# A two-layer graph attention kernel: the unmasked attention by running sums over sources sorted by f2, through DRAM by indirect DMA, in place of the 1024x1024 product

## The chip, the cores and the metric

The kernel runs on one core of one Trainium2 chip. The metric is device time in microseconds (us) of one execution. The kernel before takes 3468.1 us (median of three runs, 3465.04 to 3478.11).

## The reference, cut to what matters

There are 16 batches of 1024 nodes with 256 features, all in f32, and one adjacency matrix `adj` (1024x1024) for all. A batch passes three attentions: one unmasked inside the first layer, 512 features wide, and two masked ones, 256 wide. The unmasked one is the place of the change.

```python
def _gat(inp, adj_mask, W, a):                       # ALPHA = 0.2
    h = jnp.matmul(inp, W)
    f1 = jnp.matmul(h, a[:F_, 0])
    f2 = jnp.matmul(h, a[F_:, 0])
    e = jax.nn.leaky_relu(f1[:, :, None] + f2[:, None, :], ALPHA)
    if adj_mask is not None:
        e = jnp.where(adj_mask[None, :, :] > 0, e, NEG_INF)
    att = jax.nn.softmax(e, axis=2)
    h_prime = jnp.einsum('bij,bjf->bif', att, h)
    return jax.nn.elu(h_prime)
# layer 0, on h = relu(layernorm(x))
out = relu(h @ mlp1_w + mlp1_b)
residual = out
out = _gat(relu(out), None, W_fc, a_fc)              # unmasked, 512 wide
out = elu(out) + residual
out = relu(out @ mlp2_w + mlp2_b)
residual = out
out = _gat(relu(out), adj, W_hand, a_hand)           # masked, 256 wide
x = x + relu(elu(out) + residual)
# layer 1: x = x + relu(masked attention of relu(layernorm(x)), slope 0.01)
```

Target node i weighs source j by exp(leaky_relu(f1[i] + f2[j])). This is exp(f1+f2) where the sum is positive and exp(0.2(f1+f2)) where it isn't; each of the two is a product of a factor of i and a factor of j.

## The kernel before

A batch is held whole on the core: 1024 nodes are 8 tiles of 128 partitions (NT = 8), or 2 halves of 512 columns (NH = 2). The loop over the batches is unrolled, and the order in which an engine takes its instructions is made by the framework's scheduler from the order in which the source names them and from what is ready; it is fixed in the program. In the order of the source, batch b does this:

- `dense_attention` (L191) is the unmasked attention. It spreads f2 over all partitions by eight transposes on TensorE (`r2d`, L185), forms the row factors (`rows`) and, for each half of the targets, eight 128x512 weight tiles: ScalarE scales a row (`wd`, L222), VectorE takes the larger of the two products (`attd`, L224), and adds the tiles up for the softmax's denominator (`part`, L229). TensorE multiplies them with h (`acc`, L238): 4 chunks of 128 features by 8 sources by 2 halves. The result comes out with features on partitions, so the ELU chain (L257 to L263) adds straight into `resT`, which has that layout.
- `mlp2` (L356), `project` (`hm`, L272) and the transposes back to nodes on partitions (`on`, L368).
- `norm_transpose` and `mlp1` of batch b+1 (`nt`, L177; `m`, L329).
- `masked_attention` "a" (factors L281 to L305, weight tiles `att_a` L310, products `o_a` L318) with `finish_gnn0`, in which VectorE, ScalarE and GpSimd (`pos` L384, `e` L385) take part.
- `project_fc` of batch b+1 in two halves (`h`, L345), and between them `norm_transpose` and `project` of the second layer.
- `masked_attention` "b" (`att_b`, `o_b`) with `finish_gnn1`, whose adds are on GpSimd (L395), and the stores of the result from SyncE.

A call of an f32 matmul leaves two MATMUL records in the trace, a transpose one. DMAs are few: x in, the result out, both on SyncE's queue. GpSimd issues none.

## Time and profile before

| | |
|---|---|
| median of three runs | 3468.1 us |
| the profiled execution, its own time | 3473.71 us |
| its span (first to last instruction) | 3471.8 us |
| granted TensorE clock, mean | 0.970 |
| busy: TensorE | 3226.7 us (93%) |
| busy: VectorE, ScalarE, GpSimd | 1471.1 us (42%), 1218.5 us (35%), 375.6 us (11%) |
| moved by DMA | 43.56 MB, mean 13 GB/s |
| one batch in the steady state (two starts of `mlp2`, 1003.26 and 1216.72 us) | 213.46 us |

The busy shares are of the span. The execution's own time is 1.9 us over its span, the work around the first and the last instruction. The trace also gives the busy time in any stretch, the instructions of an engine in order of time with the idle time ahead of each in brackets, and the chain of work that ended last. Matmul ends are modelled, so matmul times here are taken from the distance of starts.

### The profile page before, as it was taken

Reading aid. Unit: us, or ns where it says so; the run is one execution under the profiler, and the core shown is the slowest. Engines: PE = TensorE matmul, PEld = TensorE weight load, DVE = VectorE, ACT = ScalarE, POOL = GpSimd, SP = SyncE. Lnnn points to the kernel's source line nnn. Section 1 sums busy time; section 2 is a strip of 40 time slices with the busy share of each in tenths; the row PEclk is TensorE's granted clock in tenths of the full one; section 3 lists DMA queues with packets and bytes.
Section 4 is the critical chain, followed back from the end, with each engine's and each line's share of the span. In section 5 each row is a group of like instructions: output and inputs, shape, how many; then the busy total and the mean of one; then the engine's idle time right before and its main releaser. Section 6 shows DMA issues by size and latency. Waiting matters only on the chain.

```text
span 3471.8 us, 32194 instructions
## 1 busy us (share of the span) xinstructions
PE 3226.7 (93%) x12161; PEld 2181.4 (63%) x12161; DVE 1471.1 (42%) x3425; ACT 1218.5 (35%) x2417; POOL 375.6 (11%) x486
## 2 busy tenths in 40 slices
PE   8899999999999999999999999999999999999997
PEld 5476574756747567475665847658476574756756
DVE  4635334353334534345343353533535334353343
ACT  3233333333333333333333334333333333333332
POOL 0010010111101111020100201101011010111102
PEclk9899999999999999999999999999999999999998
DMA  2100000000000000000000000000000000000000
GB/s 67 49 1 25 1 25 0 1 25 0 25 0 1 25 1 25 0 1 25 1 25 0 7 19 1 25 1 7 18 1 25 0 25 0 1 25 1 13 0 14
DMA packets 39635, 43.56 MB, mean 13 GB/s; under 512 B 1968, under 2 KB 36784, under 8 KB 39472
## 3 DMA queue, kind: packets, MB, share of 16 engines
q1 hardware_dynamic: 39472, 41.43, 3.6%
q8 instruction: 98, 1.61, 0.2%
q14 instruction: 65, 0.53, 0.1%
HBM read 24.64 MB, written 16.78 MB: 12 GB/s over the span
## 4 chain that ended last, share of the span: by engine, by line
PE 77%; DVE 10%; ACT 8%; POOL 2%; issue 2%; DMA 0%; ACTq 0%; POOLq 0%; DVEq 0%
PE acc L238 25%; PE o_b L318 13%; PE h L345 11%; PE m L329 6%; PE hm L272 6%; PE m L356 6%; PE o_a L318 4%; POOL e L385 2%; PE nt L177 2%; DVE att_a L310 2%; ACT pos L381 2%; PE rows L185 2%; DVE e L379 1%; ACT e L383 1%; DVE stats L163 1%
## 5 line engine op out<-in xcount | busy, mean ns | idle before, releaser
L238 PE MATMUL acc<-attd,hnat 128*128 128x512 f32 x2048 | 912.1, 602 | 0.2
L238 PEld LDWEIGHTS acc<-attd,hnat 128*128 128x128 f32 x2048 | 389.5, 194 | 464.2 <-issue 416.4
L318 PE MATMUL o_a<-hm,att_a 128*128 128x257 f32 x2048 | 478.6, 398 | 35.1 <-DVE att_a L310 35.1
L318 PEld LDWEIGHTS o_a<-hm,att_a 128*128 128x128 f32 x2048 | 408.4, 200 | 103.0 <-DVE att_a L310 39.2
L345 PE MATMUL h<-wfc_sb,resT 128*128 128x257 f32 x2048 | 453.0, 380 | 12.5 <-ACT pos L381 12.5
L318 PE MATMUL o_b<-hm,att_b 128*128 128x257 f32 x2048 | 452.9, 383 | 2.1 <-DVE att_b L310 2.1
L345 PEld LDWEIGHTS h<-wfc_sb,resT 128*128 128x128 f32 x2048 | 385.3, 189 | 75.6 <-ACT pos L381 18.6
L318 PEld LDWEIGHTS o_b<-hm,att_b 128*128 128x128 f32 x2048 | 386.6, 191 | 64.4 <-issue 4.5
L384 POOL TENSOR_TENSOR pos<-pos,onat 128x256 f32<-128x256 f32 x128 | 100.9, 789 | 1652.8 <-ACT pos L381 1505.4
L260 ACT ACTIVATE e<-e 128x512 f32<-128x512 f32 x128 | 80.7, 631 | 436.3 <-DVE e L259 436.3
L329 PE MATMUL m<-hT,w_sb 128*128 128x512 f32 x512 | 233.3, 604 | 0.0
L356 PE MATMUL m<-resT,w_sb 128*128 128x512 f32 x512 | 222.8, 592 | 0.0
L224 DVE SCALAR_TENSOR_TENSOR attd<-rowsd,bd,wd 128x512 f32<-128x512 f32 x256 | 185.7, 746 | 67.6 <-ACT wd L222 67.6
L310 DVE SCALAR_TENSOR_TENSOR att_a<-rows_a,qwd_a,edge 128x512 f32<-128x512 f32 x256 | 198.4, 831 | 31.2 <-ACT rows_a L303 31.2
L222 ACT ACTIVATE wd<-rowsd,bd 128x512 f32<-128x512 f32 x256 | 179.4, 720 | 71.2 <-DVE attd L224 70.7
L395 POOL TENSOR_TENSOR x<-x,r 128x256 f32<-128x256 f32 x128 | 109.3, 854 | 851.5 <-ACT r L394 851.5
L310 DVE SCALAR_TENSOR_TENSOR att_b<-rows_b,qwd_b,edge 128x512 f32<-128x512 f32 x256 | 188.3, 802 | 29.8 <-ACT rows_b L303 29.8
L381 ACT ACTIVATE pos<-o_a,rec 128x256 f32<-128x256 f32 x128 | 60.6, 473 | 394.2 <-DVE e L379 353.6
L394 ACT ACTIVATE r<-o_b,rec 128x256 f32<-128x256 f32 x128 | 60.6, 473 | 382.4 <-DVE rec L392 382.4
L347 ACT COPY hnat<-h 128x257 f32<-128x257 f32 x256 | 92.2, 373 | 273.1 <-PE h L345 273.1
L174 DVE TENSOR_SCALAR hn<-x,mv,rstd 128x256 f32<-128x256 f32 x256 | 95.8, 410 | 208.0 <-PE nt L177 152.7
L356 PEld LDWEIGHTS m<-resT,w_sb 128*128 128x128 f32 x512 | 97.1, 190 | 121.5 <-issue 121.5
(130 smaller groups left out, 2963.1 us busy)
## 6 DMA issues: line engine op xcount, KB each, us to landing
x<-in_x_dram SPq DMA_DIRECT2D x16, 1024.0 KB, 5.2
out_dram<-x SPq DMA_DIRECT2D x32, 512.0 KB, 2.9
adj_t<-in_adj_dram SPq DMA_DIRECT2D x16, 256.0 KB, 2.7
w_sb<-in_L_gnn_mlp_w_dram SPq DMA_DIRECT2D x2, 512.0 KB, 6.8
wfc_sb<-in_L_gnn_W_fc_dram SPq DMA_DIRECT2D x2, 512.0 KB, 6.8
wfc_sb_a<-in_L_gnn_a_fc_dram SPq DMA_DIRECT2D x1, 512.0 KB, 7.4
wh_sb<-in_L_gnn_W_hand_dram SPq DMA_DIRECT2D x1, 256.0 KB, 7.0
wl_sb<-in_L_gnn_W_dram SPq DMA_DIRECT2D x1, 256.0 KB, 7.2
```

What stands on the lines that cost most here:

```text
L222: nc.scalar.activation(w, rows[:, 1, :], AF.Copy, scale=bd[:, 1, j:j + 1])
L224: nc.vector.scalar_tensor_tensor(a_t, rows[:, 0, :], bd[:, 0, j:j + 1], w, op0=OP.mult, op1=OP.max)
L238: nc.tensor.matmul(accs[c], lhsT=h_nat[:, j, c // 2, lo:lo + P], rhs=att[j], start=(j == 0), stop=(j == NT - 1))
L272: nc.tensor.matmul(ps[:, :2 + F], lhsT=hT[:, c, t * P:(t + 1) * P], rhs=w_sb[:, c, 0, :], start=(c == 0), stop=(c == kc - 1))
L310: nc.vector.scalar_tensor_tensor(a_t, rows[:, h * HALF:(h + 1) * HALF], qwd[:, 1, j:j + 1], edge[:, j, h * HALF:(h + 1) * HALF], op0=OP.ma ...
L318: nc.tensor.matmul(ps[:, :F + 1], lhsT=att[j][:, u * P:(u + 1) * P], rhs=hm[:, j, 2:], start=(j == 0), stop=(j == NT - 1))
L329: nc.tensor.matmul(ps, lhsT=w1_sb[:, kc, c * P:(c + 1) * P], rhs=hT[:, kc, h * HALF:(h + 1) * HALF], start=(kc == 0), stop=(kc == FC - 1))
L345: nc.tensor.matmul(ps[:, :F + 1], lhsT=resT[:, kc, t * P:(t + 1) * P], rhs=wfc_sb[:, kc, g, :], start=(kc == 0), stop=(kc == HC - 1))
L356: nc.tensor.matmul(ps, lhsT=w2_sb[:, kc, c * P:(c + 1) * P], rhs=resT[:, kc, h * HALF:(h + 1) * HALF], start=(kc == 0), stop=(kc == HC - 1))
L381: nc.scalar.activation(pos, ps[:, :F], AF.Relu, scale=rec)
L384: nc.gpsimd.tensor_add(pos, pos, o_nat[:, t, :])
L395: nc.gpsimd.tensor_add(xt[:, t, :], xt[:, t, :], r)
```

## The change

The unmasked attention no longer forms the 1024x1024 weights. For each batch the sources are ordered by f2. A target's sum over sources then splits at one place k, the number of sources with f1 + f2 below zero: a running sum from the front with one factor, a running sum from the back with the other.

- `rank_and_count` spreads f2 over the partitions and counts, for each source, how many come before it (three VectorE instructions with an accumulator for each tile, two for the first). Eight indirect DMAs from GpSimd then write the rows of h (514 floats, 2056 bytes) to their places in a DRAM table `sorted_d`. ScalarE counts k by eight Sign activations with an accumulator.
- `tables` loads the sorted rows (8 consecutive rows on each partition), makes the running sums inside each partition by two chains of VectorE operations, stores them to `fine_d` (two strided DMAs), and sums over partitions by four matmuls with triangular matrices (`upto`, `after`) into `coarse_d`.
- `dense_finish` fetches for each target one row of `fine_d` and adds one row of `coarse_d` (1026 floats, 4104 bytes each) by indirect DMAs from GpSimd: for each half of the targets four that write and four that add. It then divides, combines the two sums, transposes the result (32 transposes a batch) and runs the same ELU chain into `resT`.
- The stage order is new: batch b+1's `dense_start` (projection, ranks, tables) stands ahead of batch b's masked attention "a", its `dense_finish` and `mlp2` ahead of masked attention "b". x is loaded twice, once for the norm (`xn`) and once for the residual. `resT` has two buffers; `h_nat`, `xs`, `tt` and the two `got` tiles share two slots, the tag `seq`. The masked attentions' weight tiles have 12 buffers, not 16. Their arithmetic, the MLPs and the other projections stay.

The new code in the main, and the old order at its end (`dense_attention`, which stands above, is removed):

```diff
+    upto = const.tile([P, P], F32, name="upto")
+    nc.gpsimd.memset(upto, 1.0)
+    nc.gpsimd.affine_select(out=upto, in_=upto, pattern=[[1, P]], compare_op=OP.is_ge, fill=0.0,
+                            base=0, channel_multiplier=-1)
+    after = const.tile([P, P], F32, name="after")
+    nc.vector.tensor_scalar(after, upto, -1.0, 1.0, op0=OP.mult, op1=OP.add)
...
+    sorted_d = [dram.tile([N, R], F32, name=f"sorted{k}") for k in range(2)]
+    fine_d = [dram.tile([N + 1, 2 * K], F32, name=f"fine{k}") for k in range(2)]
+    coarse_d = [dram.tile([P + 1, 2 * K], F32, name=f"coarse{k}") for k in range(2)]
...
+    def rank_and_count(h_nat, b):
+        fs = small.tile([P, 2, NT], F32, tag="fs", name=f"fs_{b}")
+        f1, f2 = fs[:, 0, :], fs[:, 1, :]
+        nc.vector.tensor_copy(f1, h_nat[:, :, 0, F])
+        nc.vector.tensor_copy(f2, h_nat[:, :, 1, F])
+        nc.gpsimd.memset(h_nat[:, :, 0, F:], 1.0)
...
+        r2_ps = bc_psum(f"r2ps_{b}")
+        row_broadcast(r2_ps, cols(f2))
+        r2 = work.tile([P, N], F32, tag="rows", name=f"r2_{b}")
+        nc.scalar.copy(r2, r2_ps)
+        rank = small.tile([P, 4, NT], F32, tag="rank", name=f"rank_{b}")
+        nc.gpsimd.memset(rank[:, 0, :], 0.0)
+        junk = work.tile([P, N], U8, tag="junk", name=f"junk_{b}", bufs=1)
+        for t in range(NT):
+            s = f2[:, t:t + 1]
+            if t:
+                nc.vector.tensor_scalar(junk[:, :t * P], r2[:, :t * P], s, None, op0=OP.is_le,
+                                        op1=OP.add, accum_out=rank[:, 0, t:t + 1])
+            nc.vector.tensor_scalar(junk[:, t * P:], r2[:, t * P:], s, None, op0=OP.is_lt,
+                                    op1=OP.add, accum_out=rank[:, 1, t:t + 1])
+            nc.vector.scalar_tensor_tensor(junk[:, t * P:(t + 1) * P], r2[:, t * P:(t + 1) * P], s,
+                                           after, op0=OP.is_equal, op1=OP.mult,
+                                           accum_out=rank[:, 2, t:t + 1])
+        nc.vector.tensor_add(rank[:, 3, :], rank[:, 0, :], rank[:, 1, :])
+        place = small.tile([P, NT], I32, tag="place", name=f"place_{b}")
+        nc.vector.tensor_add(place, rank[:, 3, :], rank[:, 2, :])
+        for t in range(NT):
+            nc.gpsimd.indirect_dma_start(
+                out=sorted_d[b % 2][:, :],
+                out_offset=bass.IndirectOffsetOnAxis(ap=place[:, t:t + 1], axis=0),
+                in_=h_nat[:, t].rearrange("p g f -> p (g f)"), in_offset=None)
+        signs = small.tile([P, NT], F32, tag="signs", name=f"signs_{b}")
+        junk2 = work.tile([P, N], mybir.dt.int8, tag="junk2", name=f"junk2_{b}", bufs=1)
+        for t in range(NT):
+            nc.scalar.activation(junk2, r2, AF.Sign, bias=f1[:, t:t + 1],
+                                 accum_out=signs[:, t:t + 1])
+        k = small.tile([P, 2, NT], I32, tag="k", name=f"k_{b}")
+        nc.vector.tensor_scalar(k[:, 0, :], signs, -0.5, N / 2, op0=OP.mult, op1=OP.add)
+        nc.vector.tensor_scalar(k[:, 1, :], k[:, 0, :], 3, None, op0=OP.arith_shift_right)
+        return top, q, k
+    def tables(top, b):
+        xs = big.tile([P, NT, R], F32, tag="seq", name=f"xs_{b}", bufs=2)
+        nc.sync.dma_start(xs, sorted_d[b % 2].rearrange("(p r) f -> p r f", p=P))
+        bd = small.tile([P, 2, NT], F32, tag="bd", name=f"bd_{b}")
+        nc.scalar.activation(bd[:, 0, :], xs[:, :, K], AF.Exp, bias=top[:, 1:2], scale=1.0)
+        nc.scalar.activation(bd[:, 1, :], xs[:, :, K], AF.Exp, bias=top[:, 2:3], scale=SLOPE_A)
+        tt = big.tile([P, NT, K], F32, tag="seq", name=f"tt_{b}", bufs=2)
+        all_t = work.tile([P, K], F32, tag="all", name=f"all_{b}", bufs=1)
+        nc.gpsimd.memset(tt[:, 0, :], 0.0)
+        nc.vector.tensor_scalar(tt[:, 1, :], xs[:, 0, :K], bd[:, 1, 0:1], None, op0=OP.mult)
+        for r in range(1, NT):
+            nc.vector.scalar_tensor_tensor(tt[:, r + 1, :] if r + 1 < NT else all_t, xs[:, r, :K],
+                                           bd[:, 1, r:r + 1], tt[:, r, :], op0=OP.mult, op1=OP.add)
+        nc.vector.tensor_scalar(xs[:, NT - 1, :K], xs[:, NT - 1, :K], bd[:, 0, NT - 1:], None,
+                                op0=OP.mult)
+        for r in range(NT - 2, -1, -1):
+            nc.vector.scalar_tensor_tensor(xs[:, r, :K], xs[:, r, :K], bd[:, 0, r:r + 1],
+                                           xs[:, r + 1, :K], op0=OP.mult, op1=OP.add)
+        fine = fine_d[b % 2]
+        nc.sync.dma_start(fine[:N, :K].rearrange("(p r) f -> p r f", p=P), tt)
+        nc.sync.dma_start(fine[:N, K:].rearrange("(p r) f -> p r f", p=P), xs[:, :, :K])
+        carry = work.tile([P, 2, K], F32, tag="carry", name=f"carry_{b}", bufs=1)
+        for s, (lhsT, total) in enumerate(((upto, all_t), (after, xs[:, 0, :]))):
+            for lo, n in ((0, F + 1), (F + 1, F)):
+                ps = mm_psum(f"carry_{b}_{s}_{lo}")
+                nc.tensor.matmul(ps[:, :n], lhsT=lhsT, rhs=total[:, lo:lo + n], start=True,
+                                 stop=True)
+                nc.scalar.copy(carry[:, s, lo:lo + n], ps[:, :n])
+        coarse = coarse_d[b % 2]
+        nc.sync.dma_start(coarse[1:P + 1, :K], carry[:, 0, :])
+        nc.sync.dma_start(coarse[:P, K:], carry[:, 1, :])
+    def dense_finish(resT, q, k, b):
+        for h in range(NH):
+            got = big.tile([P, TH, 2 * K], F32, tag="seq", name=f"got_{b}_{h}", bufs=2)
+            for u in range(TH):
+                t = h * TH + u
+                nc.gpsimd.indirect_dma_start(
+                    out=got[:, u, :], out_offset=None, in_=fine_d[b % 2][:, :],
+                    in_offset=bass.IndirectOffsetOnAxis(ap=k[:, 0, t:t + 1], axis=0))
+            for u in range(TH):
+                t = h * TH + u
+                nc.gpsimd.indirect_dma_start(
+                    out=got[:, u, :], out_offset=None, in_=coarse_d[b % 2][:, :],
+                    in_offset=bass.IndirectOffsetOnAxis(ap=k[:, 1, t:t + 1], axis=0),
+                    compute_op=OP.add)
+            qh = q[:, h * TH:(h + 1) * TH]
+            den = small.tile([P, 2, TH], F32, tag="den", name=f"den_{b}_{h}")
+            nc.vector.tensor_mul(den[:, 0, :], got[:, :, F], qh)
+            nc.vector.tensor_add(den[:, 0, :], den[:, 0, :], got[:, :, K + F])
+            nc.vector.reciprocal(den[:, 0, :], den[:, 0, :])
+            nc.vector.tensor_mul(den[:, 1, :], den[:, 0, :], qh)
+            hps = []
+            for u in range(TH):
+                part = work.tile([P, K], F32, tag="part", name=f"part_{b}_{h}_{u}")
+                nc.scalar.activation(part, got[:, u, :K], AF.Copy, scale=den[:, 1, u:u + 1])
+                hp = work.tile([P, K], F32, tag="hp", name=f"hp_{b}_{h}_{u}", bufs=TH)
+                nc.vector.scalar_tensor_tensor(hp, got[:, u, K:], den[:, 0, u:u + 1], part,
+                                               op0=OP.mult, op1=OP.add)
+                hps.append(hp)
+            for c in range(HC):
+                ps = tr_psum(f"hpT_{b}_{h}_{c}")
+                lo = c * P + (c >= HC // 2)
+                for u in range(TH):
+                    nc.tensor.transpose(ps[:, u * P:(u + 1) * P], hps[u][:, lo:lo + P], ident)
+                dst = resT[:, c, h * HALF:(h + 1) * HALF]
+                e = work.tile([P, HALF], F32, tag="e2", name=f"e_{b}_{h}_{c}")
+                nc.vector.tensor_scalar_min(e, ps, 0.0)
+                nc.scalar.activation(e, e, AF.Exp)
+                nc.scalar.activation(e, e, AF.Exp, bias=neg1)
+                nc.vector.scalar_tensor_tensor(dst, ps, 0.0, dst, op0=OP.max, op1=OP.add)
+                nc.vector.scalar_tensor_tensor(dst, e, -1.0, dst, op0=OP.add, op1=OP.add)
...
+        resT = big.tile([P, HC, N], F32, tag="resT", name=f"resT_{b}", bufs=2)
...
+    def dense_start(resT, b):
+        h_nat = project_fc(resT, b)
+        top, q, k = rank_and_count(h_nat, b)
+        tables(top, b)
+        return q, k
+    resT = mlp1(norm_transpose(x_first, 0, 0), 0)
+    q, k = dense_start(resT, 0)
+    for t in range(NT):
+        build_masks(t)
+    res_next = mlp1(norm_transpose(load_x(1, "xn"), 1, 0), 1)
+    dense_finish(resT, q, k, 0)
+    oT = mlp2(resT, 0)
+    first = weigh(project(oT, wh_sb, "hm0_0"), SLOPE_A, "a_0")
+    o_nat = natural(oT, 0)
+    for b in range(NB):
+        more = b + 1 < NB
+        resT = res_next
+        xt = load_x(b, "x")
+        if more:
+            q, k = dense_start(resT, b + 1)
+        masked_attention(first, f"a_{b}", finish_gnn0(xt, o_nat, b))
+        if b + 2 < NB:
+            res_next = mlp1(norm_transpose(load_x(b + 2, "xn"), b + 2, 0), b + 2)
+        second = weigh(project(norm_transpose(xt, b, 1), wl_sb, f"hm1_{b}"), SLOPE_B, f"b_{b}")
+        if more:
+            dense_finish(resT, q, k, b + 1)
+            oT = mlp2(resT, b + 1)
+        masked_attention(second, f"b_{b}", finish_gnn1(xt, b))
+        if more:
+            first = weigh(project(oT, wh_sb, f"hm0_{b + 1}"), SLOPE_A, f"a_{b + 1}")
+            o_nat = natural(oT, b + 1)
...
-    resT = mlp1(norm_transpose(x_next, 0, 0), 0)
-    h_nat = fc_tile(0)
-    project_fc(resT, h_nat, 0, range(NT))
-    for b in range(NB):
-        xt, more = x_next, b + 1 < NB
-        if more:
-            x_next = load_x(b + 1)
-        dense_attention(h_nat, b, resT)
-        if b == 0:
-            for t in range(NT):
-                build_masks(t)
-        hm, o_nat = mlp2(resT, b)
-        if more:
-            resT = mlp1(norm_transpose(x_next, b + 1, 0), b + 1)
-        masked_attention(hm, SLOPE_A, f"a_{b}", finish_gnn0(xt, o_nat, b))
-        if more:
-            h_nat = fc_tile(b + 1)
-            project_fc(resT, h_nat, b + 1, range(NT // 2))
-        hm = project(norm_transpose(xt, b, 1), wl_sb, FC, f"hm1_{b}")
-        if more:
-            project_fc(resT, h_nat, b + 1, range(NT // 2, NT))
-        masked_attention(hm, SLOPE_B, f"b_{b}", finish_gnn1(xt, b))
```

## The prediction

> **What bounds the kernel now.** I read the page's busy shares first, then its chain that ended last, then one batch stage by stage, then the orders of the engines and the DMA rows.
>
> ```profile
> span 3471.8 us, 32194 instructions
> PE 3226.7 (93%) x12161; PEld 2181.4 (63%) x12161; DVE 1471.1 (42%) x3425; ACT 1218.5 (35%) x2417; POOL 375.6 (11%) x486
> ...
> q1 hardware_dynamic: 39472, 41.43, 3.6%
> ...
> PE 77%; DVE 10%; ACT 8%; POOL 2%; issue 2%; DMA 0%; ACTq 0%; POOLq 0%; DVEq 0%
> ...
> L238 PE MATMUL acc<-attd,hnat 128*128 128x512 f32 x2048 | 912.1, 602 | 0.2
> ...
> x<-in_x_dram SPq DMA_DIRECT2D x16, 1024.0 KB, 5.2
> out_dram<-x SPq DMA_DIRECT2D x32, 512.0 KB, 2.9
> adj_t<-in_adj_dram SPq DMA_DIRECT2D x16, 256.0 KB, 2.7
> ```
>
> TensorE (PE) is the bound, and DMA holds 0% of the chain. `acc`, the product that goes away, is its largest group. Next, one steady batch cut at the starts of PE's stages (columns: stretch, its length, then busy time and instructions of PE, PEld, DVE, ACT, POOL, then clock and DMA).
>
> ```profile
> 1003.26:1016.99 13.73, 13.73 (x33) 6.08 (x32) 2.41 (x4) 3.41 (x5) 0.00 (x0) 1.00 0.00 0
> ...
> 1050.54:1079.84 29.30, 29.30 (x128) 25.43 (x129) 19.20 (x43) 9.29 (x22) 9.78 (x12) 0.95 0.00 1
> ...
> 1151.62:1216.72 65.10, 61.49 (x171) 29.59 (x169) 41.76 (x86) 24.87 (x38) 2.74 (x4) 0.97 0.07 25
> sum 213.46, PE 200.96 PEld 135.53 DVE 88.78 ACT 76.04 POOL 23.55; mean PE 18.27 PEld 12.32 DVE 8.07 ACT 6.91 POOL 2.14
> ```
>
> The three are `mlp2`, attention "a" and the unmasked attention. The last takes 65.10 of 213.46 us. Last, PE's order and GpSimd's (POOL) durations:
>
> ```profile
> 32.04 27.91 PE L345 MATMUL h<-wfc_sb,resT 128*128 128x257 f32 x128
> ...
> 1122.84 0.98 PE L185 MATMUL r2d<-ident,hnat 128*128 128x128 f32 x7 [1.43 <-ACT rows_b L303]
> 1123.72 28.07 PE L318 MATMUL o_b<-hm,att_b 128*128 128x257 f32 x128
> ```
>
> ```profile
> 1059.34 0.72 POOL L384 TENSOR_TENSOR pos<-pos,onat 128x256 f32<-128x256 f32 x1 [82.80 <-ACT pos L381]
> ...
> 1061.68 1.23 POOL L384 TENSOR_TENSOR pos<-pos,onat 128x256 f32<-128x256 f32 x1 [0.48 <-DVE x L386]
> ```
>
> `r2d` belongs to batch b+1, and the source names it after `o_b` of batch b: work that is ready is taken ahead of its turn. So a wait in the new stage order need not stop PE, if other work was ready when the order was made.
>
> **PE's lane after.** Removed: the 65.10 us stretch. Added: the eighth f2 transpose 0.27 (the other seven are in the stretch before, which stays); one transpose for the maximum 0.14; four carry matmuls, 8 records of 27.91/128 = 0.218, 1.7; 32 result transposes at 0.137 (`rowsps`, 8 in 1.09), 4.4. 213.46 - 65.10 + 6.5 = 154.9 us a batch. It still holds some 7 us of gaps (two waits for row factors, 4.65 and 4.74 long with 1.47 and 2.35 busy, and the transposes of the norm). If other work fills them it is 148.
>
> **The new chain through DRAM.** From the end of the projection (27.9 us) to the point where the first half's fetched tile is free:
> 1. Copies, maximum, f2 spread (1.1), its copy by ScalarE (1.01, as `rowsd` 128x1024): 3.
> 2. Ranks on VectorE. A tile compares 1024 + 128 columns in three instructions. If they run at the one-input rate (L259, 424 ns for 512), 1.0 us a tile; if at the reducing rate (L198, 1206 ns for 1024) with fixed parts of 0.15 and accumulator reads of 0.08 (the `wjunk` rows), 1.9. I take the second, since they accumulate: 15; bounds 8 and 19.
> 3. Eight scatters of 263 KB. No row shows an indirect DMA. Nearest is `adj_t`, 256 KB in 2.7 us. All eight name the whole table as destination, so I let them run one behind the other with 1 us of issue each (an assumption a little over GpSimd's 0.72 for a 128x256 add): 8 x 3.7 = 30. Bounds: pipelined 9 (2.1 MB at 331 GB/s, below, plus 2.7), or 45 if an issue takes 3.
> 4. Load of the sorted rows, 2.1 MB: queue q1 moved 41.43 MB in 3.6% of the span, 125 us, so 331 GB/s while busy; 1 MB lands in 5.2 us, so 2.1 MB in 8.4.
> 5. Two Exp 0.6 and the first scan, 7 x 0.69 + 0.43 (L262, L259): 5.9. Second scan 5.3; the first table's store hides under it.
> 6. The second store with the first one's tail: 9.5. Carries and their store, 1.7 + 1.5 + 2.7, hide under it.
> 7. Half of the fetches: 2.1 MB plain 8.4, then 2.1 MB that add to what is there. No row shows an add in flight; at plain cost 6.4 more, at three times 19 + 2. I take twice, 12.8 + 2: 23; bounds 15 and 40.
> 8. Five small divisions 0.9 and combining, 4 x 0.69, with ScalarE's part ahead: 4.5.
>
> Sum 104.6; with the projection 132.5. The five tiles of the tag `seq` share two slots, so batch b+2's projection finds a slot only when batch b+1's first `got` is used up: this chain is a lower bound of the period by itself. VectorE's 29 us in it meet other VectorE work: 88.8 - 28.7 removed, 60 of 155 us, so they stretch to 29/0.61 = 47: +18. Chain 150.
>
> GpSimd's work suffers beside VectorE. In the trace `pos` takes 0.72 us alone and 1.23 beside VectorE's `att_a`, +0.5; with 16 indirect DMAs in the chain (8 scatters, 4 + 4 fetches) that is +8 if each meets one: chain 158. The Trainium skill (SBUF — State Buffer, "Who interferes with whom" and the box on DVE and SWDGE) states that GpSimd's write of descriptors is locked out while VectorE holds the shared port pair, and has a 620 ns DMA at 3100; by that figure, as an estimate, 16 x 2.5 = 40 us would come on top and the period would be near 190. No row here shows it.
>
> **Covered.** Beside the chain PE has attention "a" 29.3, `mlp1` 19.1, norm and `hm` 10.3, attention "b" 27.9, `mlp2` and `hm` 23.5: 110, about as long as the chain after the projection, so neither lane hides wholly under the other. VectorE has 60 + 29 + 14 us, 103 of 155; ScalarE loses `wd` 11.2 and gains Sign 8 and `part` 6. If Sign needs another function table than Exp, up to 16 loads of 1.28 (the one ACT_TABLE_LOAD of the trace) make 20 us a batch on ScalarE, still under its cover of about 80. The second x load and the stores on SyncE wait behind the sorted load, which waits for the scatters; the residual x is needed only at the end of attention "a". Where VectorE waits for the sorted rows, the `att_a` tiles and the finish steps placed behind stand too, and then `o_a`; where GpSimd waits for the tables, the adds of `finish_gnn1` stand behind it.
>
> **The sum.** Lanes of 155 and 158 that lean on each other in fixed orders: I take 160 a batch. The first dense part has little to hide it: the projection ends at 59.8 (before's trace), + 104.6 + 35 for the second half = 200. Then 15 x 160 = 2400. The tail, `mlp2` of the last batch to the end, is the same work as before: 3345.94 to 3471.8, 126. With 1.9 around the span: 2728, about 2730. This stands against the profiled execution's own 3473.71, which is 0.16% over the median of the runs; I do not correct for it. Own range of this case 2550 to 3000 (periods 148 to 178).
>
> **Rivals.**
> - *DMA hides wholly* (scatters pipelined, adds at plain cost, PE's gaps filled): 170 + 15 x 148 + 128 = 2520. For: 331 GB/s busy rate, the queues nearly empty. Against: two `seq` slots. 0.12.
> - *The fixed order stalls.* The order was made for other DMA times than the chip's; VectorE and GpSimd stand at their waits, PE runs out of weight tiles. 30 us a batch: 220 + 15 x 190 + 128 = 3200. For: PE's own lane leaves no slack, and in the last batch of before PE stands 11.66 us ahead of the norm's transposes where nothing fills in. 0.18.
> - *An indirect DMA is dear*, slower than before. Place: GpSimd's queue, 24 a batch, 16 in the chain; price x us for each. Chain 97.5 + 16x a batch (150.5 less the 53 of steps 3 and 7), first part 124 + 24x, in all 1714 + 264x. It decides from x = 6.67, where this is 3475; at 8 it is 3826. For: row by row descriptors, one behind the other, an add in flight, all unseen here. Against: 256 KB in 2.7 us. 0.28.
> - No change within 0.5%, by a price between these: 0.02.
>
> **How the numbers follow.** My forecast has 0.40 and gives 2730. About 0.5% is what a measurement of this kernel can tell from no change. Faster: 0.40 + 0.12 + 0.18 = 0.70; same 0.02; slower 0.28. The range reaches from 2480 (a little under the second case) to 3700, which is x = 7.5; some 0.04 lies below and 0.14 above.
>
> **What would show it.** Right: `acc` and `wd` gone, PE near 2350 us busy (3226.7 - 16 x 61.49 + 16 x 6.5) of a span near 2730, 86%, a batch near 160 us, indirect DMAs 3 to 4 us from issue to landing, DMA moving near 20 MB a batch. The chain step by step: scatters 30, sorted load 8.4, half a fetch 23. Wrong: PE's largest idle time ahead of the result transposes or `o_a` with DMA as releaser (the chain is longer than PE's lane); POOL busy above 60% (the descriptors); table loads by the hundred; a batch over 213 us, which makes the forecast's side wrong.

## The result, and the profile after

The changed kernel takes 3905.45 us (median of four runs, 3901.62 to 3908.97) against 3470.49 us before (median of four runs, the three above among them, 3465.04 to 3478.11): a ratio of 1.1251, 95% interval 1.1226 to 1.1276. It is 12.5% slower, where 2730 us were forecast, and it lies above the range.

The page of the changed kernel: span, busy time, the two DMA queues, the group with the largest idle time on TensorE (count, then busy time and mean, then idle time before it and its releaser), and three rows of DMA issues (KB each, us to landing).

```profile
span 3904.3 us, 29961 instructions
...
PE 2515.5 (64%) x10129; PEld 1868.4 (48%) x10129; DVE 1588.5 (41%) x4098; ACT 1238.1 (32%) x2561; POOL 842.8 (22%) x920
...
q0 software_dynamic: 47104, 168.19, 17.2%
q1 hardware_dynamic: 96316, 167.56, 16.3%
...
L366 PE MATMUL carry<-all,upto 128*128 128x257 f32 (+1 forms) x64 | 33.2, 674 | 643.8 <-DVE all L352 643.8
...
xs<-sorted SPq DMA_DIRECT2D x16, 2056.0 KB, 7.6
fine<-tt SPq DMA_DIRECT2D x16, 2052.0 KB, 15.0
fine<-xs SPq DMA_DIRECT2D x16, 2052.0 KB, 20.7
```

The work did go away: TensorE (PE) is busy 2515.5 us, 711 less than before. But it stands: 64% busy, not 93%. Nearly half of the 1389 us of standing is one place, the 643.8 us ahead of the carry matmuls of `tables`, 40 us a batch. The two queues are 17.2% and 16.3% full in the mean. A mean over the span can hide full stretches: in the batch below the DMA engines are busy 0.44 of the stretch in which PE stands longest, and 0.76 of the one behind it. In the first of these PE waits for a chain of single steps, not for a full queue, as the instructions below show.

One batch, cut at PE's stages (length, then busy time and instructions of PE, PEld, DVE, ACT, POOL, then the granted clock and the DMA share):

```profile
1654.29:1681.66 27.37, 26.62 (x124) 22.83 (x123) 11.47 (x29) 10.76 (x27) 2.02 (x3) 1.00 0.00 1
1681.66:1699.06 17.40, 4.68 (x25) 2.94 (x25) 15.94 (x61) 11.96 (x21) 0.29 (x1) 0.66 0.00 0
1699.06:1748.94 49.88, 3.94 (x8) 2.68 (x9) 11.52 (x16) 2.53 (x7) 8.25 (x10) 0.50 0.44 147
1748.94:1789.64 40.70, 32.46 (x130) 26.46 (x129) 11.51 (x28) 8.10 (x19) 21.23 (x21) 0.83 0.76 169
...
sum 238.32, PE 157.24 PEld 116.31 DVE 96.76 ACT 77.24 POOL 52.87; mean PE 22.46 PEld 16.62 DVE 13.82 ACT 11.03 POOL 7.55
```

A batch takes 238.32 us, not 213.46 and not the forecast's 160. The four stretches are the projection, the ranks, the way through DRAM to the carries, and attention "a". In the second and third PE works 8.6 of 67.3 us. PE's own order in time shows why (idle time ahead of an instruction in brackets):

```profile
1697.94 1.12 PE L208 MATMUL nt<-ident,hn 128*128 128x128 f32 x4 [9.78 <-DVE hn L205]
1741.03 2.08 PE L366 MATMUL carry<-all,upto 128*128 128x257 f32 x4 [41.98 <-DVE all L352]
1747.07 2.08 PE L366 MATMUL carry<-xs,after 128*128 128x257 f32 x4 [3.97 <-DVE xs L357]
1748.94 17.41 PE L281 MATMUL o_a<-hm,att_a 128*128 128x257 f32 x72
```

The carries stand directly ahead of all of attention "a" in PE's program. When they are done, 72 records of `o_a` run without one wait. Their weight tiles had long been ready: VectorE made 12 of the 16, all that the 12 buffers hold, by 1663.9 us:

```profile
1655.91 8.02 DVE L273 SCALAR_TENSOR_TENSOR att_a<-rows_a,qwd_a,edge 128x512 f32<-128x512 f32 x12
```

PE, which could have done 17 us of work at once and the rest behind it, stood 41.98 us because its next instruction needed the running sums. VectorE and GpSimd (POOL) stand at the same chain:

```profile
1734.97 0.49 DVE L350 TENSOR_SCALAR tt<-xs,bd 128x513 f32<-128x513 f32 x1 [36.40 <-ACT bd L346]
```

```profile
1698.77 1.14 POOL L325 DMA_INDIRECT sorted<-hnat,place  x1 [18.82 <-DVE k L337]
1704.98 0.99 POOL L325 DMA_INDIRECT sorted<-hnat,place  x1 [4.94 <-DMA sorted<-hnat,place]
1708.03 0.96 POOL L325 DMA_INDIRECT sorted<-hnat,place  x1 [2.06 <-DMA sorted<-hnat,place]
...
1723.69 0.96 POOL L325 DMA_INDIRECT sorted<-hnat,place  x1 [2.50 <-issue]
...
1768.18 1.00 POOL L379 DMA_INDIRECT got<-fine,k  x1 [10.97 <-DMA fine<-xs]
```

The last of these explains most of why attention "a" takes 40.70 us where it took 29.30: the adds of `finish_gnn0` stand in POOL's queue behind the fetch, which waits for the store of the second table. VectorE stands for the adds, and `o_a` for VectorE, which has the last four weight tiles still to make:

```profile
1773.10 0.42 DVE L480 SCALAR_TENSOR_TENSOR x<-e,x 128x256 f32<-128x256 f32 x1 [11.22 <-POOL e L479]
```

```profile
1774.24 1.23 PE L281 MATMUL o_a<-hm,att_a 128*128 128x257 f32 x2 [7.89 <-DVE att_a L273]
```

That is 8.2 us, with a second wait of 0.26. The rest is that PE is busy 32.46 us there at a granted clock of 0.83, and was 29.30 at 0.95 before. The kernel before had 16 buffers for these tiles; no run here gives the new order 16, so how much of this wait they would take away is not shown.

### The profile page after: what moved, and what is told of

It reads as the page before. It is cut to its first block, busy times and chain, and to the rows that moved or that the text cites. A ratio compares the mean times of both kernels' runs of the same rounds, so it can differ in the third digit from the quotient of the medians.

```text
span 3904.3 us, 29961 instructions
## 1 busy us (share of the span) xinstructions
PE 2515.5 (64%) x10129; PEld 1868.4 (48%) x10129; DVE 1588.5 (41%) x4098; ACT 1238.1 (32%) x2561; POOL 842.8 (22%) x920
## 3 DMA queue, kind: packets, MB, share of 16 engines
q0 software_dynamic: 47104, 168.19, 17.2%
q1 hardware_dynamic: 96316, 167.56, 16.3%
## 5 line engine op out<-in xcount | busy, mean ns | idle before, releaser
L281 PE MATMUL o_a<-hm,att_a 128*128 128x257 f32 x2048 | 521.4, 417 | 132.3 <-DVE att_a L273 131.1
L366 PE MATMUL carry<-all,upto 128*128 128x257 f32 (+1 forms) x64 | 33.2, 674 | 643.8 <-DVE all L352 643.8
L208 PE MATMUL nt<-ident,hn 128*128 128x128 f32 x512 | 121.1, 351 | 303.7 <-DVE hn L205 214.0
L447 PE MATMUL m<-resT,w_sb 128*128 128x512 f32 x512 | 269.7, 670 | 57.8 <-DVE resT L413 57.8
L422 PE MATMUL m<-hT,w_sb 128*128 128x512 f32 x512 | 256.7, 660 | 61.1 <-ACT pos L475 60.2
L325 POOL DMA_INDIRECT sorted<-hnat,place x128 | 126.6, 989 | 587.0 <-DVE k L337 281.6
L208 PEld LDWEIGHTS nt<-ident,hn 128*128 128x128 f32 x512 | 72.0, 170 | 358.6 <-DVE hn L205 233.0
L384 POOL DMA_INDIRECT got<-coarse,k x128 | 214.5, 1676 | 33.2 <-issue 19.2
L422 PEld LDWEIGHTS m<-hT,w_sb 128*128 128x128 f32 x512 | 107.7, 214 | 199.0 <-issue 117.2
L480 DVE SCALAR_TENSOR_TENSOR x<-e,x 128x256 f32<-128x256 f32 x128 | 63.2, 494 | 336.7 <-POOL e L479 334.4
## 6 DMA issues: line engine op xcount, KB each, us to landing
fine<-xs SPq DMA_DIRECT2D x16, 2052.0 KB, 20.7
```

The costliest lines, as they stand in the source:

```text
L208: nc.tensor.transpose(ps[c][:, u * P:(u + 1) * P], hn[:, c * P:(c + 1) * P], ident)
L281: nc.tensor.matmul(ps[:, :F + 1], lhsT=att[j][:, u * P:(u + 1) * P], rhs=hm[:, j, 2:], start=(j == 0), stop=(j == NT - 1))
L325: nc.gpsimd.indirect_dma_start(out=sorted_d[b % 2][:, :], out_offset=bass.IndirectOffsetOnAxis(ap=place[:, t:t + 1], axis=0), in_=h_nat[:, ...
L384: nc.gpsimd.indirect_dma_start(out=got[:, u, :], out_offset=None, in_=coarse_d[b % 2][:, :], in_offset=bass.IndirectOffsetOnAxis(ap=k[:, 1 ...
L422: nc.tensor.matmul(ps, lhsT=w1_sb[:, kc, c * P:(c + 1) * P], rhs=hT[:, kc, h * HALF:(h + 1) * HALF], start=(kc == 0), stop=(kc == FC - 1))
L447: nc.tensor.matmul(ps, lhsT=w2_sb[:, kc, c * P:(c + 1) * P], rhs=resT[:, kc, h * HALF:(h + 1) * HALF], start=(kc == 0), stop=(kc == HC - 1))
```

## Experiments

Periods below are the median distance of the sorted loads of neighbouring batches in each trace; the changed kernel has 239.0 us. The theory was that the chain through DRAM has the forecast's length but that the order of the programs puts it in series with TensorE's work. The rivals: the indirect DMAs or the stores are dear in themselves, the stage order is bad by itself, GpSimd's queue is the bound.

**1. The tables behind attention "a".**

```diff
         if more:
-            q, k = dense_start(resT, b + 1)
+            top, q, k = rank_and_count(project_fc(resT, b + 1), b + 1)
         masked_attention(first, f"a_{b}", finish_gnn0(xt, o_nat, b))
+        if more:
+            tables(top, b + 1)
```

> Edit: tables() of batch b+1 is called after masked attention "a" of batch b, not before; nothing else. TensorE's program then has the products o_a ahead of the carry matmuls. Theory A (the order decides: the chain through DRAM has about the length I gave it, but ready attention work stands behind its waiting instructions): the wait ahead of carry, 42 us a batch, falls under 25, since o_a (29 us) runs in it; a batch falls from 238 to about 218, in all near 3600 us (3450 to 3700). Theory B (the path through DRAM and its two slots set the period whatever the order is): within 2% of 3905, and the wait comes back in front of the result transposes hpT.

Measured: 3561.66 us, ratio 1.0262 [1.0241, 1.0282], period 216.1. The same instructions and the same DMAs, with one call moved, are 344 us faster. The trace's waits (us in total, times, longest) show where it stands next:

```profile
DVE den L390 <- DMA got<-coarse,k: 684.4, 32, 44.5
POOL got L379 <- DMA fine<-xs: 587.1, 14, 42.7
...
PE extps_b L216 <- DVE ext_b L240: 308.3, 16, 23.1
...
PE carry L366 <- DVE all L352: 113.4, 16, 7.4
```

The wait at the carries fell from 643.8 to 113.4 us. VectorE now stands at `den`, the first step of the division, for the fetches, and the small `ext_b` queued behind it holds up attention "b".

**2. The division behind attention "b" too.** On top of 1, `dense_finish` and `mlp2` are called after the second `masked_attention`.

```diff
+        masked_attention(second, f"b_{b}", finish_gnn1(xt, b))
         if more:
             dense_finish(resT, q, k, b + 1)
             oT = mlp2(resT, b + 1)
-        masked_attention(second, f"b_{b}", finish_gnn1(xt, b))
```

> Edit: as the run before, and dense_finish and mlp2 of batch b+1 are called after masked attention "b" of batch b. Theory A: o_b (28 us) now runs while the rows are fetched; a batch near 195 us, in all near 3250 us (3100 to 3400), faster than the old kernel's 3470. Theory B: within 2% of 3905.

Measured: 3381.99 us, 0.9735 [0.9717, 0.9752], period 204.8. Already faster than before, but near the weak end of the expectation: the scheduler had still put `den` ahead of `ext_b` on VectorE.

```profile
DVE den L390 <- DMA got<-coarse,k: 676.2, 18, 44.6
...
PE extps_b L216 <- DVE ext_b L240: 316.3, 16, 23.5
```

**3. The scatters.** On the changed kernel, the eight scatters are one plain store by SyncE; the rows stay unsorted.

```diff
-        for t in range(NT):
-            nc.gpsimd.indirect_dma_start(
-                out=sorted_d[b % 2][:, :],
-                out_offset=bass.IndirectOffsetOnAxis(ap=place[:, t:t + 1], axis=0),
-                in_=h_nat[:, t].rearrange("p g f -> p (g f)"), in_offset=None)
+        nc.sync.dma_start(sorted_d[b % 2].rearrange("(t p) f -> p t f", p=P),
+                          h_nat.rearrange("p t g f -> p t (g f)"))
```

> Edit: the changed kernel in its own order, with the eight scatters of a batch replaced by one plain store of h from SyncE; the rows are then not sorted, so the output is not the attention's. This prices the scatters, which take 27.7 us from the first issue to the last landing. Theory A: TensorE waits for the chain with ready work behind it, so the time falls by all that the chain loses, 27.7 less about 9 for the plain store, 19 us a batch in 16 batches: near 3600 us (3550 to 3680). If the stretch before o_a were held by something else (VectorE's share or the clock), it would fall by less than 100 us.

Measured: 3383.83 us, 0.9737 [0.9718, 0.9756], period 205.3, 33.7 a batch less where 19 were expected. The store lands in 8.3 us and also no longer waits for the ranks: it is issued 0.3 us ahead of the first transpose of `r2ps` (1680.46 and 1680.75), where in the changed kernel the first scatter goes 17.1 us behind it (1698.77 and 1681.66). Some 37 us less of chain (17.4 of waiting for the ranks, and 27.9 from the first scatter to the issue of the sorted load, which became 8.6) gave 33.7 a batch: in the changed order, this part of the chain is paid nearly one for one. This doesn't speak for dear scatters; it shows that a piece of the chain that lies ahead of the carries counts there, whatever it is made of.

**4. GpSimd's adds.** The two adds of `finish_gnn0` go to VectorE.

```diff
-            nc.gpsimd.tensor_add(pos, pos, o_nat[:, t, :])
-            nc.gpsimd.tensor_add(e, e, pos)
+            nc.vector.tensor_add(pos, pos, o_nat[:, t, :])
+            nc.vector.tensor_add(e, e, pos)
```

> Edit: the changed kernel in its own order, with the two adds per tile of finish_gnn0 on VectorE, not GpSimd. In the trace VectorE stands 11 us a batch for an add on GpSimd that is queued behind a gather, and the gather waits for the table's store. Theory A: that stand goes, and o_a's gap of 8 us with it, but what is late next is the gather itself, whose time does not move: 5 to 10 us a batch, near 3780 us (3740 to 3850). Theory B: the same gathers land at the same time: within 1% of 3905.

Measured: 3844.92 us, 1.1078 [1.1055, 1.1101], period 235.6. The period fell by 3.4 us, less than the 5 to 10 expected, and the time lies just inside the upper edge of its range. The wait of `o_a` went, but the carries' stayed (646.1 us) and `mlp1` now waited for ScalarE (200.4 us instead of 60.2). The adds in GpSimd's queue are not the bound; the scatters and fetches stayed there.

**5. The table stores.** The two stores go to contiguous side tables, and the fetches read a table that is filled once, so they also don't wait for the stores.

```diff
-        nc.sync.dma_start(fine[:N, :K].rearrange("(p r) f -> p r f", p=P), tt)
-        nc.sync.dma_start(fine[:N, K:].rearrange("(p r) f -> p r f", p=P), xs[:, :, :K])
+        nc.sync.dma_start(side_d[0].rearrange("(p r) f -> p r f", p=P), tt)
+        nc.sync.dma_start(side_d[1].rearrange("(p r) f -> p r f", p=P), xs[:, :, :K])
```

> Edit: the changed kernel in its own order, but the two running-sum tables (2.1 MB each) are stored to two side tables with rows of 2052 bytes one behind the other, not side by side in rows of 4104 bytes; the fetches read a table that was filled once with ones, so the output is not the attention's. Price of the row layout in DRAM: I had given the second store 9.5 us and it took 20.7. If the interleaved rows are the cause, the second store lands in 8 to 11 us and the first fetch starts 10 us earlier; in this order the fetch is ahead of need but for GpSimd's adds behind it, so 5 to 12 us a batch, near 3770 us. If the two stores' bytes are the cause, both stay at 15 and 21 us and the time at 3905 within 1%.

Measured: 3890.97 us, 1.1205 [1.1186, 1.1224], period 238.1. Inconclusive on the price of a store in the chain. The DMA rows:

```profile
side<-tt SPq DMA_DIRECT2D x16, 2052.0 KB, 6.3
side<-xs SPq DMA_DIRECT2D x16, 2052.0 KB, 19.9
...
got<-fine,k POOLq DMA_INDIRECT x128, 13.5
```

The first store is contiguous on both sides and took 6.3 us instead of 15.0. The second, whose source rows are 2052 of 2056 bytes, stayed at 19.9; the fifth fetch waited for it anyway (10.51 us in POOL's order, for the slot of `seq` that `xs` holds), and the median of all fetches from the first table is 13.5 us instead of 5.4, with four of each batch started beside that store. The run also pays about 24 us once, ahead of the first sorted load, to fill the tables.

**6. The add in flight.** The fetch from `coarse_d` overwrites instead of adding, so the sums lack the parts of the earlier partitions.

```diff
-                    in_offset=bass.IndirectOffsetOnAxis(ap=k[:, 1, t:t + 1], axis=0),
-                    compute_op=OP.add)
+                    in_offset=bass.IndirectOffsetOnAxis(ap=k[:, 1, t:t + 1], axis=0))
```

> Edit: the changed kernel in its own order, with the second fetch of each target (from the coarse table) written over the first, not added; same bytes, the output is not the attention's. Price of the add: if it costs what it showed beside the plain fetch, issue goes from 1.6 to 1.0 us, landing from 7.5 to near 5.4 us, half a fetch from 22 to near 18. Theory A: the fetches are off the path in this order, so 0 to 5 us a batch, 3830 to 3905. If the fetches were the bound (theory B): 8 us a batch, near 3780.

Measured: 3809.5 us, 1.0977 [1.0959, 1.0995], period 232.5. The issue of such a fetch fell from 1676 to 1069 ns in the mean and its landing from 7.5 to 5.4 us. So an add costs 2.1 us of landing and 0.6 of GpSimd for each, 6.5 us a batch in this order: a small part of the 79 us between the forecast's period and the measured one. The time lies between what the two theories gave, so the fetches are not wholly off the path in this order.

**7. The order alone.** The old product by `acc` and `attd`, with x loaded twice and two buffers of `resT`, in the new stage order (against the kernel before: projection ahead of attention "a", the product and `mlp2` ahead of attention "b").

```diff
+            project_fc(resT, h_nat, b + 1, range(NT))
         masked_attention(hm, SLOPE_A, f"a_{b}", finish_gnn0(xt, o_nat, b))
...
+            dense_attention(h_nat, b + 1, resT)
+            oT = mlp2(resT, b + 1)
         masked_attention(hm, SLOPE_B, f"b_{b}", finish_gnn1(xt, b))
```

> Edit: the old kernel's unmasked attention (the 1024x1024 product) in the changed kernel's stage order: projection of batch b+1 ahead of masked attention a, dense attention and mlp2 ahead of masked attention b, two loads of x, two buffers of resT. One part of the change alone. Theory A: without the chain through DRAM nothing waits in the queues, TensorE stays the bound with the same work: 3470 within 1.5%. If the new order by itself costs, it is over 3550.

Measured: 3414.81 us, 0.9836 [0.9819, 0.9852]. The order is worth 1.6% to work that has no chain through DRAM. It is slow only together with the chain that it is given.

**8. The division forced behind attention "b".** On top of 2, the instructions of `dense_finish` may be placed only after the last weight tile of attention "b".

```diff
         if more:
-            dense_finish(resT, q, k, b + 1)
+            with tc.issue_after(last):
+                dense_finish(resT, q, k, b + 1)
```

> Edit: the run e2, and dense_finish's VectorE work is queued behind the last weight tile of masked attention b. In e2 TensorE waits 21 us a batch for VectorE's ext_b, which stands in VectorE's queue behind the divisions that wait for the fetched rows. Theory A: that wait goes, o_b runs while the rows come in: 3382 less 15 x 21, near 3070 us (2980 to 3200). Theory B: the rows come no earlier, the wait moves to the result transposes behind o_b: within 2% of 3382.

Measured: 3270.29 us, 0.9415 [0.94, 0.9431], period 197.3: a third of the expected gain. The wait at `extps_b` is gone, but `o_b` is slower (425 ns a record, 391 in run 2) and waits:

```profile
L281 PE MATMUL o_b<-hm,att_b 128*128 128x257 f32 x2048 | 529.1, 425 | 111.5 <-ACT r L489 75.9
```

VectorE stands at `den` again (14.07 us at 1560.32). Behind it in VectorE's order stand the reciprocals of attention "b"'s last tiles (`rec<-o_b` at 1560.81), and `o_b` waits for these through ScalarE's `r` (4.72 us at 1561.59). Only then come the 32 transposes, `mlp2`, `hm0` and the next projection, which starts at 1596.08. So the loop was still closed in series: about 160 us of chain and then 35 us of work ahead of the next chain's start. The wait that I had taken away stood beside that, not in addition to it.

**9. The next projection early.** On top of 8, the projection and the ranks of batch b+2 are called right after the division of b+1, ahead of its `mlp2`.

```diff
-        if more:
-            top, q, k = rank_and_count(project_fc(resT, b + 1), b + 1)
         masked_attention(first, f"a_{b}", finish_gnn0(xt, o_nat, b))
...
                 dense_finish(resT, q, k, b + 1)
+            if b + 2 < NB:
+                top, q, k = rank_and_count(project_fc(res_next, b + 2), b + 2)
             oT = mlp2(resT, b + 1)
```

> Edit, on top of the divide-behind-b kernel: the projection and the ranks of batch b+2 are called right after the fetches and divisions of batch b+1, ahead of its mlp2, instead of at the top of the next turn; so ranks, scatters, sorted load and scans of the next batch run while TensorE does mlp2, hm0 and attention a. Theory A (the loss is serial: about 35 us of hpT, mlp2 and hm0 stand between the end of one chain of 160 us through DRAM and the start of the next, which gives the period of 195; the chain itself has the length that was predicted): the period falls to 165 to 180, total 200 + 15 x 170 + 128 = 2880 (2800 to 3030). Theory B (the engines' work at the lowered TensorE clock, 2538.5 us busy or 159 a batch, and the waits inside the attention stages already set the 195 us): within 2% of 3270.

Measured: 2879.23 us, 0.8281 [0.8265, 0.8297], period 168.7, where 2880 and 170 were expected. Page of this kernel, and one batch of it:

```profile
span 2879.2 us, 30248 instructions
...
PE 2424.8 (84%) x10129; PEld 1823.1 (63%) x10129; DVE 1595.4 (55%) x4098; ACT 1238.4 (43%) x2561; POOL 876.2 (30%) x920
```

```profile
1500.00:1668.70 168.70, 150.00 (x629) 113.52 (x629) 97.19 (x247) 77.13 (x160) 55.66 (x57) 0.93 0.49 125
```

The operations are those of the changed kernel; the order of four calls differs, with the division held back as in run 8, and 1026 us are gone. PE's order around the chain is now this:

```profile
1581.82 16.64 PE L437 MATMUL h<-wfc_sb,resT 128*128 128x257 f32 x76
...
1600.42 13.04 PE L448 MATMUL m<-resT,w_sb 128*128 128x512 f32 x30
...
1663.71 1.03 PE L367 MATMUL carry<-all,upto 128*128 128x257 f32 x4
```

The projection stands ahead of `mlp2`, and the first carries, behind attention "a", start without a wait in this batch. The ranks are counted beside `mlp2`; the scatters go out from 1615.68 to 1638.20, beside `hm0` and the start of attention "a"; the second scan ends at 1670.1, the second store runs beside `mlp1`, and the fetches (from 1690.21 on) beside the second layer's `hm` and attention "b".

**10. Run 9 with the adds of run 4.**

> The same, and the two adds of finish_gnn0 are VectorE's instead of GpSimd's, so that no add stands between the eight scatters (in the divide-behind-b kernel the scatters were issued at 1644.36 to 1669.05, 24.7 us, with eight adds of 0.72 among them). Theory A: with the projection early the scatters run beside mlp2 and hm0, not beside attention a, so the adds no longer meet them; within 1% of the kernel without this edit, a little slower if VectorE's 16 x 0.5 us a batch count. Theory B (GpSimd's queue is what the chain hangs on wherever it stands): 4 to 8 us a batch faster, 60 to 130 us.

Measured: 2852.82 us, 0.8203 [0.8184, 0.8221], period 167.7. A gain of 0.9%: theory A's size, but not its reason. In run 9 the first adds of `finish_gnn0` wait behind the last scatter (POOL):

```profile
1638.20 0.96 POOL L326 DMA_INDIRECT sorted<-hnat,place  x1 [2.51 <-issue]
1640.99 0.53 POOL L350 MEMSET tt<- 128x513 f32 x1 [1.83 <-DMA sorted<-hnat,place]
1641.48 0.71 POOL L479 TENSOR_TENSOR pos<-pos,onat 128x256 f32<-128x256 f32 x1
```

and `o_a`, which began at 1625.96, runs out of weight tiles (99.0 us of waits for `att_a` in all). Without the adds on POOL it is 18.1. So the scatters met the adds after all, and what suffered was attention "a", not the chain. Most of the waits that went came back elsewhere: ahead of the carries 162.6 us in all, 106.9 in run 9, and for VectorE at `den` 182.8, 131.5 in run 9. This version is the fastest that ran with the full computation, 18% under the kernel before.

**11. Run 9 with the plain store of run 3** (rows unsorted).

> Edit, on top of the kernel with the early projection: the eight scatters are one plain store by SyncE that doesn't wait for the ranks (rows not sorted; ranks still computed), the same edit that took 32.8 us a batch from the changed kernel by shortening the chain by about 35 us. Theory A (with the early projection the chain of 150 to 154 us lies beside TensorE's work of the same batch and no longer sets the period): of the 35 us only the two waits before the carry matmuls (4.9 and 5.7 us) and a part of attention a's waits can go, 5 to 12 us a batch, 2700 to 2800. Theory B (the chain through DRAM still sets the period, 169 us, as its bound of 150 plus contention): 25 to 35 us a batch, 2320 to 2480.

Measured: 2778.73 us, 0.8004 [0.799, 0.8017], period 163.9. The edit that took 33.7 us a batch from the changed order takes 4.8 here. Of the rest, the first batch gains 41 us, as its sorted load goes out at 69.3 instead of 110.3 us, and the end gives part of it back (248.6 us from the last sorted load to the end, 223.0 in run 9). What VectorE still waits for fetched rows (us in total, times, longest), run 9 and then this run:

```profile
DVE den L391 <- DMA got<-coarse,k: 131.5, 17, 37.1
```

```profile
DVE den L388 <- DMA got<-coarse,k: 10.4, 2, 5.7
```

With the chain this much shorter it has left the path, all but a little. With the scatters kept it has not: in run 10 DMAs hold 27% of the chain of work that ended last and PE 37%, in run 11 16% and 54%.

## Why the prediction was wrong

**The chain had nearly the forecast's length.** In the batch shown (all in us, forecast then measured): preparation 3, 3.4; ranks 15, 13.6; scatters 30, 27.7 (mostly 3.0 apart, each behind the landing of the one before); sorted load 8.4, 7.7; Exp and first scan 5.9, 6.6; second scan 5.3, 6.0; second store 9.5, 20.7; half a fetch 23, 22.4; combining 4.5, 7. From the end of the projection to the free tile 104.6 was summed and 116.7 measured (1680.9 to 1797.6), with the projection 132.5 and 147.7. The store was mis-sized by 11 us. The 18 us for VectorE's other work and the 8 for GpSimd beside it were not to be seen: ranks and scans ran at their bare cost, because the engines had nothing else ahead of them. So 158 was forecast and 147.7 came. That these are near is partly luck: 26 us of allowances did not come in this order, and 15 that nobody forecast did (11 in the store, 2.5 in the combining, 3 in the projection, some less elsewhere).

**The step that failed is "Covered", and with it the 160 of "The sum".** There I set TensorE's 110 us of other work beside the chain and took the longer of the two lanes. That needs two things of the order: that PE's program has other work where the chain is waited for, and that the next chain starts while the last stages of this batch still run. Neither held. The source calls `tables` ahead of attention "a", the carries are PE instructions, and an engine takes its instructions in their fixed order; so of the 110 us only attention "a", a part of the norm and the first 3.6 us of `mlp1` lay beside the chain, attention "a" behind the carries at that. And the projection of the next batch is called after `mlp2`, attention "b" and `hm0`. The batch was therefore a sum: 147.7 of chain and 91 of work that begins when the chain has ended. My inference from `r2d`, which the scheduler had taken ahead of `o_b`, was too wide: it had put one small ready group forward, and I read from it that the whole of `o_a` would be put ahead of the carries. Run 1 shows this step by itself (22.9 us a batch), run 9 the other (28.6 from run 8).

**The rivals.** The second one named the mechanism, fixed orders that stall, but priced it at 30 us a batch on top of 160, and that number had no working. The measured period less the forecast's is 239 - 160 = 79, and run 9 took 239.0 - 168.7 = 70.3 of it away by order alone. The rival of dear indirect DMAs covers the measured time and is still not what happened: a scatter costs 3.6 us from issue to issue in the mean ((1723.69 - 1698.77)/7) and a half's eight fetches (1790.56 - 1768.18)/8 = 2.8, where it needed 6.67 to decide; at 3.2 its formula gives 2559. The signs named under "wrong" were the right ones: a batch over 213 us, and PE's largest idle time at the chain, though ahead of the carries, which I had not listed.

**PE's lane.** Forecast 2350 us busy; measured 2515.5, and 2402.0 in run 10 on the same instructions. The difference goes with the clock, and most with the groups that stand behind waits. The clock granted was 1.00 in the projection, 0.66 in the stretch with the 9.78 us wait, 0.50 in the stretch with the 41.98 us wait and 0.83 in attention "a" behind it. A record of `o_a` took 417 ns where it took 398 before, one of `mlp1`'s `m` 660 where it took 604, while `h` and `o_b` kept their price (379 and 381, before 380 and 383). A batch that is 157.24 us of PE work in the changed order is 150.00 in run 9, at 0.93. I had costed waits as if the work after them kept its price. Beside that, the new small groups were mis-sized: the carries take 4.2 us a batch (2 x 33.2/16) where 1.7 was counted, and the transposes `hpT` 5.9 (94.5/16) where 4.4 was. The Trainium skill (TensorE: Matmul & The Clock Gate, "Why this matters for your kernels") warns of gaps over about 3 us between bursts of matmuls. The rows above, with their gaps of 9.78 and 41.98 us, agree with it.

**The lock of the shared port.** The prediction's 2.5 us more for each of 16 DMAs was an estimate. The page's figure behind it (the Trainium skill, SBUF — State Buffer, "A bandwidth-pool intuition that's wrong (but worth ruling out)") is for a DMA of about 620 ns that takes about 3100 beside a `tensor_copy` of VectorE. No run here puts such a copy beside a scatter. What the runs show is scatters beside VectorE's `att_a`, which is a `scalar_tensor_tensor`. In run 9 three were issued beside ten of these tiles in a row (1625.15 to 1631.87): one held GpSimd 0.96 us like the others, two 1.30 and 1.21, and the steps behind those two were 3.40 and 3.23 us where 3.0 to 3.2 is usual. That is some 0.3 us and not 2.5. The median fetch landed in 7.1 us in run 9, where it took 5.4 in the changed kernel; other DMAs and VectorE's work both lie beside it, and no run separates them.

**What became of the forecast.** With the order changed in runs 9 and 10, the period is 168 against 160 and the time 2879 and 2853 against 2730. That is 5.5 and 4.5% over in time, for an order that the forecast did not have. In run 9 PE's lane is 150.0 us of work and 18.7 of waits, where 148 and 7 were forecast; the waits are largest at the carries (106.9 us in all) and at attention "a" (99.0). The chain is 167.1 us there, from the first record of the projection (1566.34) to the end of the first half's combining (1733.48), nearly the whole period. It is longer than the 147.7 of the changed order because its steps now meet other work: the scans take 19.2 us (1650.91 to 1670.1) where they took 12.1, with VectorE's work for attention "a" among them. So the allowances for sharing, which did not come in the changed order, come where the lanes run side by side. The prediction's sum is near the measured one for such an order, not shown to be exact in each term.

## What to carry to other kernels

A long chain and a busy engine cost the longer of the two only if the busy engine's program holds other work at every point where it meets the chain; write out each engine's order around the chain's first and last instruction, and where the next chain can start, before taking a maximum. If a few instructions of the busy engine belong to the chain, everything behind them waits as long as they do, so call them late; and call the work that starts the next chain as early as its inputs and buffers allow. A queue that is 17% full and an engine that is 64% busy were here a hint that the order was at fault and not the price of the parts. The hint alone proves nothing, as such means hide full stretches; runs 1 and 9, which change the order alone, showed it.

## What the runs showed of the hardware

- A scatter of 263 KB by row addresses landed in 2.7 us and held GpSimd for 0.96 us; a fetch of 525 KB took 5.4 and 0.97; one that adds in flight 7.5 and 1.68. These are near what the prediction took: 27.7 us for the scatters of a batch, where it took 30, and 22.4 for half a fetch, where it took 23.
- A store of 2.1 MB in pieces of 2052 bytes, 4104 apart in DRAM, took 15.0 and 20.7 us, where a load of the same size took 7.7 and a store contiguous on both sides 6.3. Why the second one is so slow stays open: other DMAs ran beside it in each run.
- Sign with an accumulator brought no function table load: the trace after has one ACT_TABLE_LOAD, as before.
